# Later bias additions on the residual, and a later turn of the bias vectors, in a cross-attention block

## The chip, the cores and the metric

The kernel runs on one core of one Trainium2 chip. The metric is the device time in microseconds of one execution; lower is better. The engines are TensorE (PE in the profile; PEld is its weight load), VectorE (DVE), ScalarE (ACT), GpSimd (POOL) and SyncE (SP), which issues nearly all DMAs.

## The reference, cut to what matters

All data are float32. There are 8 sequences of 256 tokens, for the queries and for the context, and the width is 512.

```python
x = layer_norm(hidden, ln1_w, ln1_b)
q = x @ q_w + q_b            # 16 heads of 32
k = enc @ k_w + k_b
v = enc @ v_w + v_b
a = softmax(q @ k.T / sqrt(32), where(mask))  @ v
hidden = a @ cproj_w + cproj_b + hidden_states
y = layer_norm(hidden, ln2_w, ln2_b)
y = gelu(y @ fc_w + fc_b)    # 512 -> 2048
out = hidden + y @ proj_w + proj_b
```

## The kernel before

**Tiling.** Two sequences form a group of 512 tokens, so there are four groups, g = 0 to 3. Each matrix product is done in quarters of 256 by 256, named "11", "12", "21" and "22", by a Strassen scheme of seven products in place of eight (`strassen`, `fc`, `proj`); sums of quarters (`sum_up`, L171, `A_SUMS` for weights and `B_SUMS` for tokens) are made ahead of it on POOL and DVE. The first product of the keys of group 0 is the exception: `eight` makes each quarter by plain products, 16 recorded matmuls in two halves i = 0 and 1.

**No scheduler.** The order of the source is the order of the instructions on each engine. Each engine works off its own list in that order.

**Start.** Contexts, key weights, x and the other weights are loaded by SP. Eight small loads on POOL's queue bring the bias and norm vectors into `rows`, as rows. `turn_cols` turns them on PE into `ps_cols` (L476) and DVE copies them to `cols` (L477), the per-partition scalars that nearly every later step uses: the keys' bias in `made` (ACT, L437), the norm's scale in `turn_x`. The source calls `turn_cols` after the products of quarter "11". The order that follows is: turn the second half of the context (`pct`), quarter "12" (`pkT_12`), statistics of x on DVE (L194, L195), `roots` on POOL (L199, L200), quarter "21", the norm on DVE (L203), the transposes of x (`pxt`), quarter "22", then the queries (`pqT`).

**Attention.** It has 32 units, n = 0 to 31: eight per group, u = 0 to 7, each with four heads of one sequence. Unit n computes scores two units ahead, softmax on DVE and ACT, the division by the sums on POOL one unit ahead (`divide(n + 1)`, L599, `pr`, which waits for `rsum`, L597), turns the probabilities on PE (`ppt`, L610) and multiplies them by the values (`av`, L626). The lists `between` and `aside` hold other work for places inside a unit: `begin(g, u, i, f, ...)` puts f at place i of unit u of group g, where i = 0 to 2 lie before `attend` and i = 3 is the end of the unit. In these places the projections of the next group, the norms and the output projection (`project_out`, `po`) are woven in.

**The residual in the attention.** `load_res(g, n)` loads a quarter of x into `resx` by SP. The output projection adds its result to that tile on POOL (L541), and SP stores it to `hid_dram` (L542). For quarter "12" `load_res` also adds the difference `cbd` of two halves of the bias, on POOL (L534), in the same call as the load. Group 0's quarters are loaded at the end of unit 8, group 1's "12" at the end of unit 22, group 2's at the end of unit 28, and group 3's after unit 31.

**The MLP.** For each group, four steps q = 0 to 3 make a quarter of the hidden layer each: seven products (`pf`, L903), sums on DVE, GELU on ACT (L966), then two sums on POOL (L1007, L1008). In group 0, step q also makes the weight sums `fcw[q + 1]` of the following step on POOL. Step 0 loads the residual `resm` from `hid_dram` (1 MB, `residual`), adds two bias terms to halves of it on POOL (L1014), and loads the next group's tokens `hm` (`load_hid`). In group 0 SP issues this load after the four quarters of `proj_w` (`pw`, 1 MB each). After step 3 come the statistics of `hm` on DVE, `ve_m` and `rstd_m` on POOL, the norm on DVE (L203), and the output products (`proj`, `py`), between which `hm` is turned (`pyt`, `turn_next`). POOL makes sums for them (L1058, L1067), DVE empties the first product's bank (L1052), and the residual enters at L1064, L1075, L1080, L1083 and L1087.

Of the kernel before, what the change touches and what calls it, by code (L numbers as in the profile page):

```python
# [13 lines left out]
ALU = mybir.AluOpType  # L14
# [8 lines left out]
def tile_xattn_block(  # L23
# [45 lines left out]
    nc = tc.nc  # L69
# [6 lines left out]
    NG = B // GB  # L76
# [9 lines left out]
    HI, HC, HF, HD2 = INNER // 2, NC // 2, NF // 2, D // 2  # L86
# [37 lines left out]
    def col(base, i):  # L124
        return cols[:, base + i : base + i + 1]
# [42 lines left out]
    def sum_up(eng, x, table, *which):  # L168
        for i in which:
            to, a, b, op = table[i]  # L170
            eng.tensor_tensor(x[to], x[a], x[b], op)  # L171

    def load_tiles(pool, src, tag, name, between=None):
        tiles = []
        for t in range(NT):
            if between and t == NT // 2:
                between()
            xt = pool.tile([P, D], F32, tag=tag, bufs=NT, name=f"{name}_{t}")
            nc.sync.dma_start(xt, src[ts(t, P), :])
            tiles.append(xt)  # L180
        return tiles

    def group_of(x, g):
        return x[g * G : (g + 1) * G, :]
# [44 lines left out]
    def residual(pool, src, tag, name):  # L229

        t = pool.tile([P, NT, D], F32, tag=tag, bufs=1, name=name)
        nc.sync.dma_start(t, src.rearrange("(t p) d -> p t d", p=P))
        return t
# [3 lines left out]
    def load_hid(g):  # L237
        hids[g] = load_tiles(both, hid_dram[g], "xt", f"hm_{g}")
# [10 lines left out]
    with ExitStack() as att:  # L249
        work = att.enter_context(tc.tile_pool(name="attwork", bufs=2))  # L250
        cb = work.tile([P, D], F32, tag="cb", bufs=1, name="cb")
        cbd = work.tile([P, S], F32, tag="cbd", bufs=1, name="cbd")
# [4 lines left out]
        mbias, ctxT, xnT, vs, qk, probs, stats, res = ({} for _ in range(8))  # L257
# [16 lines left out]
        def turned(name):  # L274


            places[0] += 1
            if not pts and (places[0] % 2 or probs):
                return ps_t.tile([P, G], F32, tag="pt", name=name)
            return ps_s.tile([P, G], F32, tag="s", name=name)  # L280
# [64 lines left out]

            return [lambda c=c: piece(c) for c in range(NC)]

        turns, later = [0], []

        def strassen(name, a, b, weight_moves, made, bias=None):  # L350

# [103 lines left out]
        def eight(name, n, w, x, made):  # L455


            bank = ps_m.tile([P, 2, S], F32, tag=f"m{turns[0]}", name=f"{name}_{n}")
            turns[0] ^= 1
            for i in range(2):  # L460
                for c in range(NC):
                    nc.tensor.matmul(  # L462
                        bank[:, i, :],
                        w[f"{n[0]}{c // HC + 1}"][:, c % HC, ts(i, P)],
                        x()[f"{c // HC + 1}{n[1]}"][:, c % HC, :],
                        start=i == 0 and c == 0,
                        stop=c == NC - 1,
                        skip_group_check=True,
                    )
            if n == "11":  # L470
                turn_cols()
            made(n, bank, None)

        def turn_cols():
            ps = turned("ps_cols")
            nc.tensor.transpose(ps[:, :n_rows], rows, ident[:n_rows, :n_rows])  # L476
            nc.vector.tensor_copy(cols, ps[:, :n_rows])  # L477
# [41 lines left out]
        def by_tiles(row):  # L519
            return row[:, None, :].to_broadcast([P, 2, S])  # L520

        def quarter_of(src, n):

            o, k = int(n[0]) - 1, int(n[1]) - 1
            return src[k * S : (k + 1) * S, ts(o, S)].rearrange("(t p) d -> p t d", p=P)

        def load_res(g, *which):
            for n in which:
                r = work.tile([P, 2, S], F32, tag=f"res{n}", bufs=1, name=f"resx_{g}_{n}")
                nc.sync.dma_start(r, quarter_of(group_of(xf, g), n))  # L530
                res[g, n] = r
                if n == "12":

                    nc.gpsimd.tensor_tensor(r, r, by_tiles(cbd), ALU.add)  # L534

        def project_out(g):
            def made(n, bank, u):
# [119 lines left out]
        def begin(g, u, i, f, *args):  # L657
            aside[g, u, i].append(lambda: f(*args))
# [44 lines left out]
        def share(g, pieces, plan):  # L703

            pieces = list(pieces)
            for u, i, n in plan:
                between[g, u, i] += pieces[:n]
                del pieces[:n]
            assert not pieces
# [37 lines left out]
        spread(0, [(6, 2), (6, 2), (7, 2), (7, 2)], [lambda i=i: sum_up(GP, ws["c"], A_SUMS, i) for i in ALL])  # L747
        g = 1
        begin(g, 0, 3, load_res, 0, *QUARTERS)
        g = 2  # L750
        begin(g, 0, 3, spill_att, 1)
        begin(g, 5, 3, reload_att, 1)
        sums_at(att_in, 1, [(g, 6, 1), (g, 6, 2), (g, 7, 1), (g, 7, 2)])
        begin(g, 5, 3, load_res, 1, "11", "22", "21")
        begin(g, 6, 3, load_res, 1, "12")
        g = NG - 1
        share(
            g,
# [3 lines left out]
        for u, h, which in (  # L762
            (2, 2, ("11",)), (3, 2, ("22", "21")), (4, 2, ("12",)), (5, 3, ("11",)), (7, 3, ("22", "21"))
        ):
            begin(g, u, 3, load_res, h, *which)

        begin(g, 0, 0, load_hid, 0)
        norm_over(
# [20 lines left out]
        def run(pieces):  # L789
            for p in pieces:  # L790
                p()
# [19 lines left out]
        k, q, v, tx = project_qk(0, "kT"), project_qk(0, "qT"), project_v(0), turn_x(0)  # L811
# [67 lines left out]
        for i in ALL:  # L879
            run(o[i : i + 1])  # L880
            sum_up(V, ys[0], B_SUMS, i)
        run(o[4:])
        run(later)
        load_fc(3)
# [2 lines left out]
    with ExitStack() as mlp:  # L887
# [39 lines left out]
        for g in range(NG):  # L927
# [28 lines left out]
            for q in range(HF // 2):  # L956
                bank = {
                    n: ps_f.tile([P, 2, S], F32, tag=f"f{n}", name=f"pf{n}_{g}_{q}") for n in (1, 6, 7, 5)
                }
                u1 = work.tile([P, 2, S], F32, tag="u1", bufs=1, name=f"u1_{g}_{q}")  # L960
                u2 = work.tile([P, 2, S], F32, tag="u2", bufs=2, name=f"u2_{g}_{q}")
                u3 = work.tile([P, 2, S], F32, tag="u3", bufs=1, name=f"u3_{g}_{q}")

                def gelu(n, half, src):
                    for i in range(2):
                        nc.scalar.activation(  # L966
                            h[n][q][:, i, :],
                            src[:, i, :],
                            AF.Gelu_apprx_tanh,
                            bias=col(c_fcb, half * HF + 2 * q + i),  # L970
                            scale=1.0,
                        )

                ahead = g == 0 and q + 1 < HF // 2

                def some_pw(n):
                    if g == 0 and q:
                        for _ in range(n):
                            next(pw_sums)

                fc(bank[1], "11", "11", q, True, False)
                nc.scalar.copy(u1, bank[1])  # L982
                fc(bank[6], "s2", "t2", q, True, True)
                nc.vector.tensor_tensor(u2, bank[6], u1, ALU.add)
                fc(bank[7], "s3", "12", q, True, False)
                nc.vector.tensor_tensor(u3, bank[7], u2, ALU.add)
                fc(bank[5], "21", "t1", q, True, False)
                nc.vector.tensor_tensor(h["22"][q], bank[5], u3, ALU.add)
                if ahead:
                    sum_up(nc.gpsimd, fcw[q + 1], A_SUMS, 0, 1)  # L990
                some_pw(1)
                fc(bank[1], "12", "21", q, False, True)

                gelu("11", 0, bank[1])
                gelu("22", 1, h["22"][q])
                fc(bank[7], "22", "t4", q, False, True)
                nc.vector.tensor_tensor(h["12"][q], bank[7], u2, ALU.add)
                if ahead:
                    sum_up(nc.gpsimd, fcw[q + 1], A_SUMS, 2, 3)
                some_pw(2)  # L1000
                gelu("12", 1, h["12"][q])
                fc(bank[5], "s4", "22", q, False, True)
                nc.vector.tensor_tensor(h["21"][q], bank[5], u2, ALU.add)  # L1003
                some_pw(1)
                gelu("21", 0, h["21"][q])

                nc.gpsimd.tensor_tensor(h["s3"][q], h["11"][q], h["21"][q], ALU.subtract)  # L1007
                nc.gpsimd.tensor_tensor(h["21"][q], h["21"][q], h["22"][q], ALU.add)  # L1008
                if q == 0:
                    ht = residual(work, hid_dram[g], "resm", f"resm_{g}")  # L1010

                    for b, bias in ((0, projb[:, :HD2]), (1, pbd)):
                        o = out_quarter(b, 0)
                        nc.gpsimd.tensor_tensor(o, o, by_tiles(bias), ALU.add)  # L1014
                    if g + 1 < NG:
                        load_hid(g + 1)

            if g + 1 < NG:
                seen, roots, normalise = layer_norm(hids[g + 1], f"m{g + 1}")
# [3 lines left out]
            bank = {  # L1023
                n: ps_f.tile([P, 2, HD2], F32, tag=f"f{n}", name=f"py{n}_{g}") for n in (1, 6, 7, 5)
            }
# [104 lines left out]
```

## Time and profile before

| what | value |
|---|---|
| median of 3 runs | 768.07 us (766.93 to 768.81) |
| profiled execution, its own time | 769.02 us |
| span of that execution, first to last instruction | 767.2 us |
| PE busy | 749.7 us, 98% of the span |
| POOL, DVE, ACT busy | 378.3, 360.5, 293.0 us |
| mean granted PE clock | 0.993 |
| moved by DMA | 68.70 MB |

The span is what the engines' instructions cover. The difference of 1.8 us between span and time lies around it. A line of a timeline has start, duration, engine, source line, operation, output and inputs, shape and count; a bracket at its end gives the engine's idle time before it and what ended that. A line of waits has the waiting engine and line, what it waited for, then total, number and longest. PE's busy time has modelled ends, so consecutive pieces overlap by some 0.16 us.

### The profile page before, as it was taken

The page shows a single profiled execution, that of the slowest core. Times are in us where ns is not written, and L with a number is a line of the kernel's source. Part 1 is how long each engine was busy: PE and PEld are TensorE (multiplying, and loading weights), DVE is VectorE, ACT ScalarE, POOL GpSimd, SP SyncE. Part 2 cuts the span into 40 slices and gives each one's busy share as a digit, 9 for nine tenths or more (in the row PEclk, how much of TensorE's full clock was granted, in tenths as well). Part 3 has the DMA queues.
Part 4 walks back from the last instruction along what each step waited for, and adds up shares of the span by engine and source line. Part 5 has one row for each costly group of instructions (what it writes and reads, how often), then busy time and mean ns, then how long its engine had stood idle before and what let it go on. Part 6 is the DMA issues. An engine that isn't in the chain of part 4 may idle for free.

```text
span 767.2 us, 12111 instructions
## 1 busy us (share of the span) xinstructions
PE 749.7 (98%) x4437; PEld 628.9 (82%) x4437; DVE 360.5 (47%) x970; ACT 293.0 (38%) x851; POOL 378.3 (49%) x346
## 2 busy tenths in 40 slices
PE   8999999899999999999979999999999999999997
PEld 7888777688888777768858888888888888888886
DVE  3676756566466566765325641225512264122111
ACT  2277787655776777761313001330004210032100
POOL 3856779467564569986472530315403245022340
PEclk9999999999999999999989999999999999999999
DMA  9614432632234358333920004000031000110001
GB/s 302 223 56 147 147 111 84 187 119 83 83 101 152 96 180 283 116 97 98 309 102 1 1 0 152 14 0 1 1 100 65 1 1 0 59 52 0 1 1 55
DMA packets 60331, 68.70 MB, mean 90 GB/s; under 512 B 5060, under 2 KB 46064, under 8 KB 60144
## 3 DMA queue, kind: packets, MB, share of 16 engines
q1 hardware_dynamic: 60016, 67.91, 27.2%
q8 instruction: 35, 0.57, 0.3%
q14 instruction: 24, 0.20, 0.1%
q0 software_dynamic: 256, 0.02, 0.0%
HBM read 46.95 MB, written 20.97 MB: 89 GB/s over the span
## 4 chain that ended last, share of the span: by engine, by line
PE 84%; POOL 6%; issue 3%; DMA 2%; ACT 2%; DVE 1%; SPq 1%; POOLq 0%; DVEq 0%
PE py L903 25%; PE pf L903 23%; PE ppt L610 5%; PE pqT L367 5%; PE pkT L367 5%; PE pv L367 5%; PE po L367 5%; PE s L557 4%; PE av L626 4%; POOL pr L599 3%; DMA resm<-hid_dram 2%; PE pkT L462 1%; ACT pr L585 1%; PE pxt L216 1%; PE pyt L216 1%
## 5 line engine op out<-in xcount | busy, mean ns | idle before, releaser
L903 PE MATMUL pf<-y,fcw 128*128 128x256 f32 x896 | 196.9, 383 | 5.7 <-POOL fcw L171 5.7
L903 PEld LDWEIGHTS pf<-y,fcw 128*128 128x128 f32 x896 | 172.0, 192 | 30.0 <-POOL fcw L171 6.1
L599 POOL TENSOR_TENSOR pr<-pr,rsum 128x512 f32<-128x512 f32 x128 | 130.1, 1048 | 68.3 <-DVE rsum L597 44.8
L585 ACT ACTIVATE pr<-pr,nmax 128x256 f32<-128x256 f32 x256 | 128.1, 503 | 61.3 <-DVE nmax L575 61.2
L575 DVE CUSTOM_DVE_ANT_0 pr<-s,mb 128x256 f32<-128x256 f32 x256 | 94.0, 412 | 42.1 <-PE s L557 35.0
L1007 POOL TENSOR_TENSOR hs<-h,h 128x512 f32<-128x512 f32 x16 | 20.3, 1270 | 181.2 <-PE pf L903 139.0
L903 PE MATMUL py<-pw,h 128*128 128x256 f32 x384 | 84.8, 379 | 0.0
L903 PE MATMUL py<-pw_t,h 128*128 128x256 f32 x384 | 83.5, 379 | 0.0
L903 PEld LDWEIGHTS py<-pw,h 128*128 128x128 f32 x384 | 72.7, 190 | 9.8
L903 PEld LDWEIGHTS py<-pw_t,h 128*128 128x128 f32 x384 | 72.7, 190 | 9.8
L982 ACT COPY u<-pf 128x512 f32<-128x512 f32 x16 | 9.4, 586 | 165.9 <-PE pf L903 164.6
L610 PE MATMUL ppt<-ident,pr 128*128 128x128 f32 x512 | 69.1, 277 | 3.3 <-POOL pr L599 3.3
L610 PEld LDWEIGHTS ppt<-ident,pr 128*128 128x128 f32 x512 | 57.2, 141 | 18.4 <-issue 9.1
L966 ACT ACTIVATE h<-pf,cols 128x256 f32<-128x256 f32 x32 | 13.4, 470 | 108.3 <-PE pf L903 108.3
L615 ACT COPY pt<-ppt 128x512 f32<-128x512 f32 x96 | 51.6, 571 | 7.9 <-PE ppt L610 7.9
L966 ACT ACTIVATE h<-h,cols 128x256 f32<-128x256 f32 x96 | 43.4, 501 | 25.8 <-DVE h L1003 13.3
L367 PE MATMUL pqT<-xnT,qw 128*128 128x256 f32 x224 | 52.6, 388 | 0.0
L367 PE MATMUL pv<-vw,ctxT 128*128 128x256 f32 x224 | 52.4, 380 | 0.0
L585 ACT ACTIVATION_READ_ACCUMULATOR pr<-pr,nmax 128x1 f32 x256 | 48.5, 189 | 0.0
L367 PEld LDWEIGHTS pqT<-xnT,qw 128*128 128x128 f32 x224 | 42.5, 195 | 5.4
L367 PEld LDWEIGHTS pv<-vw,ctxT 128*128 128x128 f32 x224 | 41.0, 190 | 5.4 <-issue 0.3
L626 PE MATMUL av<-pt,v 128*32 128x256 f32 x512 | 38.9, 386 | 1.3 <-ACT pt L615 0.4
(132 smaller groups left out, 964.8 us busy)
## 6 DMA issues: line engine op xcount, KB each, us to landing
ctx<-in_ctx_dram SPq DMA_DIRECT2D x16, 256.0 KB, 4.3
x<-in_x_dram SPq DMA_DIRECT2D x16, 256.0 KB, 3.9
v_dram<-st_v SPq DMA_DIRECT2D x16, 256.0 KB, 2.2
v<-v_dram SPq DMA_DIRECT2D x16, 256.0 KB, 3.8
resx<-in_x_dram SPq DMA_DIRECT2D x16, 256.0 KB, 5.1
hid_dram<-resx SPq DMA_DIRECT2D x16, 256.0 KB, 2.2
hm<-hid_dram SPq DMA_DIRECT2D x16, 256.0 KB, 6.0
fcw<-in_L_xattn_fc_w_dram SPq DMA_DIRECT2D x16, 256.0 KB, 6.0
```

Of the source, the lines that this page charges most:

```text
L216: nc.tensor.transpose(ps[:, ts(t, P)], xt[:, ts(c, P)], ident)
L367: nc.tensor.matmul(bank[n][:, i, :], l[:, c, ts(i, P)], r[:, c, :], start=first and i == 0 and c == 0, stop=last and c == HC - 1, skip_gro ...
L557: nc.tensor.matmul(banks[j][:, i, :], qT[j * HD : (j + 1) * HD, b * S + i * P : b * S + (i + 1) * P], kT[j * HD : (j + 1) * HD, b * SK : ( ...
L575: nc.vector.tensor_tensor_reduce(pr[:, j, i, :], banks[j][:, i, :], mbias[g][1][:, b, :], scale=-SCALE, scalar=FLT_MAX, op0=ALU.add, op1=A ...
L585: nc.scalar.activation(pr[:, j, i, :], pr[:, j, i, :], AF.Exp, bias=nmax[:, j, i : i + 1], scale=-1.0, accum_out=sums[:, j, i : i + 1],)
L599: nc.gpsimd.tensor_tensor(pr[:, j], pr[:, j], rsum[:, j, :, None].to_broadcast([P, NQ, SK]), ALU.mult,)
L610: nc.tensor.transpose(ps[:, kc, ts(i, P)], probs[n][:, j, i, ts(kc, P)], ident)
L615: nc.scalar.copy(pt, ps)
L626: nc.tensor.matmul(av[j * HD : (j + 1) * HD, :], vs[g, hg][:, b * NK + kc, ts(j, HD)], pts[n, j][:, kc, :], start=(kc == 0), stop=(kc == N ...
L903: nc.tensor.matmul(ps, lhsT, rhs, start=first, stop=last, skip_group_check=True)
L966: nc.scalar.activation(h[n][q][:, i, :], src[:, i, :], AF.Gelu_apprx_tanh, bias=col(c_fcb, half * HF + 2 * q + i), scale=1.0,)
L1007: nc.gpsimd.tensor_tensor(h["s3"][q], h["11"][q], h["21"][q], ALU.subtract)
```

## The change

Three things move, and nothing is computed otherwise. Firstly, the addition of `cbd` to `resx` "12" leaves `load_res` for a function of its own, `bias_res`, called one or more units later (for group 3: after the fourth product of its output projection). Secondly, in the MLP the two additions of the bias to `resm` go from step 0, behind the load, to step 3; the loads stay in step 0. Thirdly, `turn_cols` is called between the two halves of the keys' quarter "12", and only then quarter "11" gets its bias.

```diff
-        turns, later = [0], []
+        turns, later, waiting = [0], [], []
...
             for i in range(2):
+                if n == "12" and i == 1:
+
+                    turn_cols()
+                    waiting.pop()()
                 for c in range(NC):
                     nc.tensor.matmul(
...
             if n == "11":
-                turn_cols()
-            made(n, bank, None)
+                waiting.append(lambda: made(n, bank, None))
+            else:
+                made(n, bank, None)
...
                 res[g, n] = r
-                if n == "12":
-
-                    nc.gpsimd.tensor_tensor(r, r, by_tiles(cbd), ALU.add)
+
+        def bias_res(g):
+
+            r = res[g, "12"]
+            nc.gpsimd.tensor_tensor(r, r, by_tiles(cbd), ALU.add)
...
         begin(g, 0, 3, load_res, 0, *QUARTERS)
+        begin(g, 2, 2, bias_res, 0)
...
         begin(g, 6, 3, load_res, 1, "12")
+        begin(g, 7, 3, bias_res, 1)
...
             begin(g, u, 3, load_res, h, *which)
+        begin(g, 6, 2, bias_res, 2)
...
             sum_up(V, ys[0], B_SUMS, i)
+        bias_res(3)
         run(o[4:])
...
                 if q == 0:
                     ht = residual(work, hid_dram[g], "resm", f"resm_{g}")
+                    if g + 1 < NG:
+                        load_hid(g + 1)
+                if q == HF // 2 - 1:
 
                     for b, bias in ((0, projb[:, :HD2]), (1, pbd)):
                         o = out_quarter(b, 0)
                         nc.gpsimd.tensor_tensor(o, o, by_tiles(bias), ALU.add)
-                    if g + 1 < NG:
-                        load_hid(g + 1)
```

## The prediction

> **What bounds the kernel now.** I read the page's busy shares first, then who TensorE (PE) waits for, then the timelines around each of those waits.
>
> ```profile
> PE 749.7 (98%) x4437; PEld 628.9 (82%) x4437; DVE 360.5 (47%) x970; ACT 293.0 (38%) x851; POOL 378.3 (49%) x346
> ```
>
> PE is the bound: it is idle for only 767.2 - 749.7 = 17.5 us. So an edit pays only where PE pauses, or where it runs slowly. The waits of PE alone:
>
> ```profile
> PE pf L903 <- POOL fcw L171: 5.7, 1, 5.7
> PE ppt L610 <- POOL pr L599: 3.3, 5, 2.0
> PE warm L796 <- POOL neg_half L110: 1.4, 1, 1.4
> PE ps_cols L476 <- DMA rows<-in_L_xattn_fc_b_dram: 1.1, 1, 1.1
> ```
>
> Three of the four belong to what the change touches. POOL's timeline (start, duration, line, last the idle time before) says why POOL was late with `fcw`, in MLP group 0:
>
> ```profile
> 377.29 1.27 POOL L1008 TENSOR_TENSOR h<-h,h 128x512 f32<-128x512 f32 x1
> 388.65 1.26 POOL L1014 TENSOR_TENSOR resm<-resm,projb 128x512 f32<-128x512 f32 x1 [10.09 <-DMA resm<-hid_dram]
> 389.87 1.26 POOL L1014 TENSOR_TENSOR resm<-resm,pbd 128x512 f32<-128x512 f32 x1
> 391.08 5.17 POOL L171 TENSOR_TENSOR fcw<-fcw 128x512 f32<-128x512 f32 x4
> ```
>
> The bias adds on `resm` wait 10.09 us for a load that SP issued behind 4 MB of `pw`; the `fcw` sums for the third step stand behind them. The same picture in unit 8 to 10 of the attention, where the add on `resx_12` stands ahead of the softmax divisions:
>
> ```profile
> 149.60 1.27 POOL L534 TENSOR_TENSOR resx<-resx,cbd 128x512 f32<-128x512 f32 x1 [9.64 <-DMA resx<-in_x_dram]
> 150.82 8.03 POOL L599 TENSOR_TENSOR pr<-pr,rsum 128x512 f32<-128x512 f32 x8
> ```
>
> A pause costs more than its length. In the windows (busy time of each engine, then the granted PE clock) PE is fully busy after each pause, but at a little over half rate:
>
> ```profile
> 149.00:153.00 4.00, 1.68 (x21) 1.04 (x15) 2.33 (x9) 1.36 (x5) 3.40 (x4) 1.00 0.57 193
> 153.00:157.00 4.00, 4.00 (x13) 3.32 (x14) 1.05 (x6) 1.57 (x5) 4.00 (x5) 0.57 0.95 339
> ...
> 394.00:400.00 6.00, 6.00 (x17) 4.82 (x18) 0.69 (x1) 0.00 (x0) 5.92 (x5) 0.58 0.00 0
> 400.00:406.00 6.00, 6.00 (x30) 5.28 (x29) 2.83 (x5) 1.63 (x4) 4.26 (x4) 1.00 0.00 0
> ```
>
> **What the Trainium skill says.** "TensorE: Matmul & The Clock Gate", Part 1, says that an idle array drops to half clock and needs a busy window of about 3.4 us to return. The trace agrees on the size (0.57, 0.58), but here a pause of some 2 us followed by a shorter one was enough. The same page (the note on queue depths) calls GpSimd's queue strict FIFO: agreed, the `fcw` sums waited behind `resm`. "SBUF — State Buffer", Who interferes with whom, says that a VectorE tensor_scalar in its two-port mode and a GpSimd instruction exclude each other: agreed, L203 takes 1.48 us beside POOL's L1058 and 0.54 us at 17.2, where POOL is idle.
>
> **The change part by part.** No DMA is issued in another order. Moved are 4 adds on `resx_12`, 8 on `resm`, one transpose with its copy, and two activations.
>
> *MLP.* The two adds go from step 0 to step 3. After L1008 ends at 378.5 POOL runs the four `fcw` sums (5.17) by 383.7; PE asks for the first of them at 388.0. The next ones follow L1007/L1008 of step 1, whose input ACT finishes at 388.0, so they are half done at about 393 against a need at 400.1. So nothing is late next. Gain: in the chain of work PE needs, from 362.10 to 419.08, 56.98 us for the four steps; in a group without a pause 48.35 (469.18 to 517.52). That is **8.63**: 5.74 of pause and 2.89 of half clock.
>
> Cost: in step 3 the adds (2 x 1.24 = 2.48) now stand before `ve_m`, `rstd_m` and L1058 in all four groups. Group 1:
>
> ```profile
> 521.85 0.23 POOL L199 TENSOR_SCALAR ve_m<-mv_m 128x4 f32<-128x4 f32 x1
> ...
> 523.24 5.71 DVE L203 TENSOR_SCALAR hm<-hm,mv_m,rstd_m 128x512 f32<-128x512 f32 x4 [1.78 <-POOL rstd_m L200]
> 528.87 0.68 DVE L1052 TENSOR_TENSOR v<-py,projb 128x512 f32<-128x512 f32 x1
> ```
>
> L203 now ends at 528.95 + 2.48 = 531.43; PE transposes `hm` from 531.17 and wants the last tile, after three transposes of 0.11, at 531.50. L1052 ends at 532.03, and PE reuses its bank at 532.05. So cover is used up to the last 0.05; in group 0, with 2.22 of delay (POOL had waited 0.26 for `mv_m`), L1052 ends at 433.7 against 433.6. I take 0.3 for three groups; bounds 0 and 1.5 (0.5 each). The delayed L1058 ends at 531.1 and is needed at 539.8; group 3 has no norm. DVE's `pw` sums and copies queued behind L203 in group 0 end at 437.6, needed at 440.5.
>
> *Attention, `resx_12` of group 0.* Its add goes behind `rstd_a` of unit 10. Then the divisions of unit 10 run once `rsum` is there (141.4) and end at 145.4, for a need at 149.7. What PE loses now: the transposes should have led to the first matmul of `pkT` 1.73 after 150.66, at 152.39; it came at 156.82. Gain **4.43**, of it 1.58 half clock (3.31 for 8 matmuls that take 1.73). The add itself (1.27) falls at about 160.7 to 162.0 on the new time scale, before the next `rsum` (166.5 - 4.4 = 162.1). Its load, landed at 149.6, is no issue.
>
> *Group 2's `resx_12`* (unit 28 to unit 30): before, POOL stood from 332.49 to 334.90 for it (the page blames DVE's `nmax`, but the load issued at 331.53 took 3.3 us), and PE then waited 0.56 in unit 30 and 0.33 + 0.56 in unit 31 for divisions. Afterwards they start 3.6 us sooner. Gain **1.45**. Group 1's add had waited 0.6 with no pause of PE: nothing. Group 3's add waited 7.4 at 358.5 under the last `po` products; PE had no pause there, so nothing, only that the last store goes some 0.5 sooner.
>
> *Start.* The bias transpose moves into the second key quarter. PE saves the 1.06 wait for `rows`: `pkT_12` starts about 11.2 instead of 12.55. But its copy to `cols` now waits for half of that product (11.2 + 1.73 + 0.27), and `bn_stats` of x stands behind it on DVE:
>
> ```profile
> 12.41 0.68 DVE L194 BATCH_NORM_STATS2 st_a<-x 128x6 f32<-128x512 f32 x1
> ...
> 17.18 1.92 DVE L203 TENSOR_SCALAR x<-x,mv_a,rstd_a 128x512 f32<-128x512 f32 x4 [1.49 <-POOL rstd_a L200]
> ```
>
> So the norm starts at 13.27 and ends at 19.96 instead of 19.10. PE is ready at 18.3 and transposes x as it comes, to end at 21.4 (before: 21.3). The 1.06 saved turn into a wait for DVE. I take **+0.1**; bounds -0.5 (the norm's chain shrinks) and +1.7 (the pause trips the clock). The two activations end at 14.3, before `pkT_21` needs their bank at 14.8.
>
> Sum: -8.63 - 4.43 - 1.45 + 0.3 + 0.1 = -14.1. The profiled execution took 769.02 (1.82 around its span); it becomes 754.9. It stands 0.95 above the median of 768.07, so I forecast **754.0**.
>
> **The rivals.**
> - *The start trips the clock.* Of the 1.7 us from 18.3, some 1.4 are idle. For it: about 2 us did at 149.9. Against: 1.06 and 0.35 close together at 9.9 to 12.5 did not. Price +1.6: 755.6.
> - *A moved wait isn't the one that ends last*, so that the change does not do what it says at that place: a late `rsum` or a filled queue keeps the divisions back (758.4 without the 4.43), or the `fcw` sums are late for another reason (762.6 without the 8.63). For it: the page's releasers are inferred, and one of them is wrong here. Against: the sums' start is the adds' end in the timelines.
> - *Slower: the adds and `bn_stats` exclude each other* at each end of a group. Then `ve_m` is late by 2.48 and another 4 x 0.66, 5.1 in all; with a cover of 2.3 PE pauses 2.8, and the clock adds up to 2.9: 5.7 in three groups, 17.1 against 14.5 won: 770.8. It decides from 4.8 per group on. Against: L1007 and L1008 already run beside `bn_stats` (518.2 to 521.4) at 1.27 and 0.66, as alone.
>
> **How the numbers follow.** The forecast 0.75 (its own range 752.5 to 755.5: 1.0 for the spread of 766.93 to 768.81, 0.5 for the start), the start 0.12, a wait that stays 0.10, slower 0.03. The range 752.5 to 759.0 takes in the first two and the 758.4. About 0.3%, 2.3 us, is what a measurement of this kernel can tell from no change: faster 0.95, same 0.02, slower 0.03.
>
> **What would show it.** Right: no PE wait for `fcw`, PE clock 1.0 through steps 1 to 3 of MLP group 0, about 48.4 from its first `pf` to its first `py`; no PE pause at 149 and 337 to 345; in the first 25 us, PE waiting for `x` from L203 in place of `rows`; L203's end within 0.1 of the `pyt` transposes. Wrong: a wait of PE for `hm` or `pyt` over 0.5 per group, POOL's adds above 1.5, a clock under 0.9 near 20.

## The result: 11.5 us faster

The changed kernel takes **756.0 us** (median of 4 runs, 755.8 to 756.3) against 767.5 us before (4 runs beside it, 766.9 to 768.8). The ratio is 0.985, 95% interval 0.983 to 0.987: 11.5 us less, between 10 and 13. The profiled executions differ a little more: their spans are 767.2 and 754.0 us, 13.2 apart.

Parts 1 and 4 of the page of the changed kernel, the busy times and the shares of the chain that ended last:

```profile
PE 745.0 (99%) x4437; PEld 625.1 (83%) x4437; DVE 361.2 (48%) x970; ACT 293.4 (39%) x851; POOL 380.2 (50%) x346
...
PE 94%; ACT 2%; DVE 2%; issue 1%; DMA 1%; POOL 0%; SPq 0%; DVEq 0%; POOLq 0%
```

PE has the same 4437 matmuls and is idle for 9.0 us where it was for 17.5. It is also busy for 4.7 us less with the same work: for the most part that is half clock that is gone. POOL's work has not shrunk (380.2 against 378.3), but its share of the chain rounds to 0%. What PE alone waits for now:

```profile
PE warm L806 <- POOL neg_half L110: 1.4, 1, 1.4
PE pkT L466 <- DMA kw<-in_L_xattn_k_w_dram: 0.9, 1, 0.9
...
PE pxt L216 <- DVE x L203: 0.2, 1, 0.2
```

The waits for `fcw`, for `pr` and for `rows` are off the list. In their place stands a short one for `x`. POOL's timeline in the first steps of MLP group 0 shows why; the `fcw` sums follow the sums of their own step at once:

```profile
372.28 1.27 POOL L1019 TENSOR_TENSOR h<-h,h 128x512 f32<-128x512 f32 x1
373.51 5.65 POOL L171 TENSOR_TENSOR fcw<-fcw 128x512 f32<-128x512 f32 x4
```

The same windows as before, which had 0.57 and 0.58 in the column of the granted clock (the second pair lies some 5 us further on in the work, since group 0 starts 5.0 sooner):

```profile
149.00:153.00 4.00, 4.00 (x34) 3.44 (x35) 3.57 (x15) 2.59 (x9) 0.93 (x1) 1.00 0.55 169
153.00:157.00 4.00, 4.00 (x24) 3.59 (x23) 3.75 (x14) 2.74 (x9) 3.12 (x4) 1.00 0.80 287
...
388.00:394.00 6.00, 6.00 (x29) 5.28 (x28) 4.29 (x6) 2.54 (x6) 3.24 (x3) 1.00 0.00 0
394.00:400.00 6.00, 6.00 (x30) 5.28 (x29) 2.15 (x4) 1.49 (x3) 2.53 (x2) 1.00 0.00 0
```

PE is busy for all of each window, at full clock. For the sum I cut the span at fixed pieces of PE's work. The same cuts serve for the experiments: the start up to the first `pqT`; from the scores that PE computes within unit 10 (those of unit 12) to the ones within unit 16; from the scores computed within unit 29 (the last ones) to the first `pf`; the four steps of MLP group 0; and the output products of groups 0, 1 and 2 with the norm between them (first `py` to the next `pf`).

| kernel (span, us) | start | unit 10 to 16 | unit 29 to `pf` | steps of group 0 | `py` of groups 0, 1, 2 |
|---|---|---|---|---|---|
| before (767.2) | 24.76 | 68.03 | 32.81 | 56.98 | 50.09, 50.10, 50.10 |
| after (754.0) | 24.98 | 63.75 | 31.83 | 48.35 | 50.30, 50.22, 50.21 |
| difference | +0.22 | -4.28 | -0.98 | -8.63 | +0.21, +0.12, +0.11 |
| predicted | +0.1 | -4.43 | -1.45 | -8.63 | +0.3 in all |

The differences add up to -13.2, the whole of the spans' difference.

### The profile page after: what moved, and what is told of

The parts are those of the page before. It is cut to its first block, busy times and chain, and to the rows that moved or that the text cites. A ratio compares the mean times of both kernels' runs of the same rounds, so it can differ in the third digit from the quotient of the medians.

```text
span 754.0 us, 12115 instructions
## 1 busy us (share of the span) xinstructions
PE 745.0 (99%) x4437; PEld 625.1 (83%) x4437; DVE 361.2 (48%) x970; ACT 293.4 (39%) x851; POOL 380.2 (50%) x346
## 4 chain that ended last, share of the span: by engine, by line
PE 94%; ACT 2%; DVE 2%; issue 1%; DMA 1%; POOL 0%; SPq 0%; DVEq 0%; POOLq 0%
PE py L914 26%; PE pf L914 26%; PE ppt L617 7%; PE pqT L367 6%; PE pv L367 5%; PE po L367 5%; PE s L564 5%; PE av L633 5%; PE pkT L367 5%; ACT pr L592 2%; PE pkT L466 1%; PE pyt L216 1%; PE pxt L216 1%; ACT pt L622 1%; PE pct L216 1%
## 5 line engine op out<-in xcount | busy, mean ns | idle before, releaser
L914 PE MATMUL pf<-y,fcw 128*128 128x256 f32 x896 | 194.0, 379 | 0.0
L914 PEld LDWEIGHTS pf<-y,fcw 128*128 128x128 f32 x896 | 170.2, 190 | 23.1
L367 PE MATMUL pqT<-xnT,qw 128*128 128x256 f32 x224 | 51.0, 379 | 0.0
```

The costliest lines, as they stand in the source:

```text
L367: nc.tensor.matmul(bank[n][:, i, :], l[:, c, ts(i, P)], r[:, c, :], start=first and i == 0 and c == 0, stop=last and c == HC - 1, skip_gro ...
L914: nc.tensor.matmul(ps, lhsT, rhs, start=first, stop=last, skip_group_check=True)
```

## The experiments

The theory is that of the prediction: additions at the head of POOL's queue held up the sums and divisions that PE needed, each pause made PE run on at half clock, and nothing else decides the time. Its rivals: the half-clock stretch has a cause of its own; the additions and `bn_stats` hold each other up; the start matters in itself.

### One part at a time

Three kernels that take over one part each, the others as before.

**e1_mlp_only**: only the additions on `resm` move.

```diff
-                if q == 0: [adds on resm]
+                if q == HF // 2 - 1: [adds on resm]
```

> The kernel before with the MLP part alone: the adds on resm go to step 3. Theory (the pause for fcw and the half clock behind it go, the norm's cover at the ends of groups 0 to 2 is just used up): span 8.63 - 0.43 = 8.2 us shorter than before, about 759; group 0 from first pf to first py 48.4, then 0.1 to 0.2 more per group before the fourth output product. Rival (part of the 8.63 belongs to the earlier stores and loads that the attention part brings): the pause shrinks but stays, 3 to 6 us won, and PE still waits for fcw or hs.

Measured: 760.7 us (758.8 to 761.4), ratio 0.989 (0.986 to 0.993), 7.1 less than the kernel before beside it (767.7), where 8.2 was expected. The steps of group 0 take 48.35, as in the whole change. The profiled execution is the fastest of the four (758.8), and in it unit 10 to 16 takes only 65.52 although nothing was changed there; its clock held at 1.00 behind that pause, as it does in e12 below.

**e2_resx_only**: only the additions on `resx` "12" move (`bias_res`).

```diff
-                if n == "12":
-                    nc.gpsimd.tensor_tensor(r, r, by_tiles(cbd), ALU.add)
+        begin(g, 2, 2, bias_res, 0)   # and groups 1, 2, 3
```

> The kernel before with bias_res alone, at its four places. Theory: unit 10 gains 4.3 and units 30 and 31 gain 1.0, so the span is 5.3 shorter, about 762, and the pause for fcw with its half clock stays at 8.6. Rival (the gain in units 30 and 31 is the 1.45 of the forecast, and was only lost again elsewhere): 5.9 shorter.

Measured: 763.6 us (763.0 to 765.8), ratio 0.995 (0.993 to 0.996), 4.1 less. Unit 10 to 16 takes 63.75 and the last units 31.83, as in the whole change; group 0's steps still 56.58. So both gains are there in the profile (4.28 and 0.98, the 5.3 that was expected), while the medians show 1.2 less; the two gains are taken against the first profile of before, in which unit 10 lost its full price (e12).

**e3_cols_only**: only `turn_cols` moves.

```diff
+                if n == "12" and i == 1:
+                    turn_cols()
+                    waiting.pop()()
```

> The kernel before with the later turn of the bias vectors alone. Theory (the wait for rows becomes a wait for the norm of x, since the copy to cols stands ahead of bn_stats on DVE): the first pqT starts at about 25.1 in place of 24.9, span within 0.3 of before. Rival (the wait for kw that the run after showed at 5.9 hid a gain of 0.9): first pqT at about 24.2, 0.7 shorter.

Measured: 768.2 us (765.7 to 770.1), ratio 1.000 (0.998 to 1.002). The first `pqT` came at 25.51. In the profiled executions with the old order it came at 24.76, 25.15, 25.23, 25.27 and, in e2_resx_only, at 27.13; with the new order at 24.98 to 25.80, so no sooner. The third part moves the median by nothing that can be told. The one late start is half clock again. PE's timeline and a window of e2_resx_only:

```profile
11.63 0.23 PE L476 MATMUL ps_cols<-ident,rows 44*128 44x44 f32 x1 [1.54 <-DMA rows<-in_L_xattn_fc_b_dram]
...
13.23 8.86 PE L462 MATMUL pkT<-ctxT,kw 128*128 128x256 f32 x32 [0.35 <-DVE ctxT L324]
```

```profile
13.00:17.00 4.00, 3.77 (x10) 3.10 (x11) 3.24 (x9) 0.51 (x1) 0.44 (x2) 0.59 1.11 338
```

The wait for `rows`, 1.54 here, is followed by products at 0.59, which take 8.86 for 7.17. So the old order could lose 1.7 at this place when `rows` came late; none of the profiled executions with the new order did.

The two parts that pay give 7.1 + 4.1 = 11.2 of the 11.5. These medians are known to within some 2.7 and 1.4 us only; that neither part hides the other is shown by the stages, each of which is as short with one part alone as in the whole change.

### Is the half clock the pause's doing?

**e4_before_fill**: the kernel before, with 40 transposes of the identity into an unused bank, in the place where PE pauses for `fcw`. They are work that the output doesn't need.

```diff
                 nc.scalar.copy(u1, bank[1])
+                if g == 0 and q == 2:
+                    dummy = ps_m.tile([P, G], F32, tag="mm", name="dummy")
+                    for t in range(40):
+                        nc.tensor.transpose(dummy[:, ts(t % NT, P)], ident, ident)
```

> The kernel before with 40 transposes of the identity on PE, into a bank that nobody reads, ahead of the second product of step 2 in MLP group 0, where PE pauses 5.74 us; they take about 4.3 us. Theory (the slow matmuls after the pause are the clock that drops because PE idles): with the pause filled the clock stays at 1.0, no slow matmuls, span 2.9 shorter though PE does more. Rival (they are slow for what runs beside them, POOL's sums or the loads of weights just made): still 2.9 of slow matmuls, span as before within 0.5.

PE's timeline there, and the windows of the same kernel:

```profile
388.23 4.53 PE L986 MATMUL dummy<-ident 128*128 128x128 f32 x40
393.16 9.12 PE L903 MATMUL pf<-y,fcw 128*128 128x256 f32 x41 [0.40 <-POOL fcw L171]
```

```profile
388.00:394.00 6.00, 5.60 (x46) 5.19 (x45) 0.07 (x1) 1.00 (x3) 5.82 (x5) 1.00 0.15 56
394.00:400.00 6.00, 6.00 (x30) 5.28 (x29) 2.73 (x4) 0.00 (x0) 5.84 (x6) 1.00 0.00 0
```

`fcw` comes 4.93 us after PE has done all that it could do without it (393.16 - 388.23), yet the clock stays at 1.00 and the steps of group 0 take 53.38, against 56.58 to 56.98 in the kernels with the bare pause. With 40 more instructions PE is 3.2 to 3.6 us sooner. Not all of that is clock: the bare pauses are a little longer, 5.11 to 5.74 (before, e2, e3, e12). What these four lose beyond the pause, against 48.35, is 2.7 to 3.1 us; in e4 it is 0.1 (53.38 - 48.35 - 4.93). So the half clock comes from PE standing idle, not from what it runs afterwards. The total follows in part: 765.8 (763.4 to 767.6), ratio 0.997 (0.995 to 0.998), 1.9 less than before; what became of the rest I did not find.

### How much cover is left, and do the additions and `bn_stats` collide?

**e8_four_adds**: the changed kernel with each addition on `resm` followed by one more of the same size into a spare tile, whose result is not used.

```diff
                         nc.gpsimd.tensor_tensor(o, o, by_tiles(bias), ALU.add)
+                        nc.gpsimd.tensor_tensor(spare, o, by_tiles(bias), ALU.add)
```

> The changed kernel with each add on resm in step 3 followed by one more of the same size into a tile that nobody reads: 2.5 us more on POOL at the end of each group. Theory (the cover of the norm is used up by the first 2.5): all of it shows, PE stops 2.4 to 2.5 us before the pyt transposes in groups 0 to 2, 7.4 in all, and the clock drops behind stops of that length, 1.6 to 2.9 more each: span 9 to 16 longer than the changed kernel. Rival (there is still cover): under 4 longer, clock 1.0.

The waits of PE alone (first line), two windows at the end of group 0, and PE's first products after that:

```profile
PE pyt L216 <- DVE hm L203: 6.5, 6, 1.1
```

```profile
419.00:423.00 4.00, 1.85 (x11) 1.11 (x10) 4.00 (x4) 0.00 (x0) 3.20 (x3) 1.00 0.00 0
423.00:427.00 4.00, 4.00 (x13) 3.25 (x12) 3.92 (x7) 0.00 (x0) 0.00 (x0) 0.57 0.00 0
```

```profile
423.19 8.76 PE L914 MATMUL py<-pw,h 128*128 128x256 f32 x32
```

Two more additions of 1.27 make every group 4.3, 4.3 and 4.1 us longer (54.61, 54.47, 54.27 in place of 50.30, 50.22, 50.21): 6.5 / 3 = 2.2 of waiting, and then the clock; 32 products take 8.76 where they took 7.17. The median is 767.2 us (765.1 to 769.4), ratio 1.000: **the whole gain is gone**. The first two additions had used up nearly all of the cover. The mechanism of the slower rival had no place to act. POOL's and DVE's timelines at the end of group 0:

```profile
409.01 1.27 POOL L1020 TENSOR_TENSOR h<-h,h 128x512 f32<-128x512 f32 x1
409.57 0.66 DVE L194 BATCH_NORM_STATS2 st_m<-hm 128x6 f32<-128x512 f32 x1
410.24 1.27 POOL L1029 TENSOR_TENSOR resm<-resm,projb 128x512 f32<-128x512 f32 x1
```

The last `bn_stats` ends at 410.23, and the first addition on `resm` starts at 410.24; in groups 1 and 2 too the additions come after them all. What does run beside `bn_stats` is the pair of sums ahead of the additions (L1019, L1020), and neither is slowed: 1.27 and 0.66.

**e5_adds_step2**: the additions of the changed kernel one step earlier, in the third step (`if q == 2:`), where POOL has room and the load has long landed.

> The changed kernel with the adds on resm in step 2 in place of step 3. Theory (the adds in step 3 delay the norm by 2.5 us, 0.1 more than its cover): PE's stops at the pyt transposes and at the third output product go, 0.43 shorter in the span, L203 ends 2.5 earlier against PE; resm has landed by then, so POOL does not wait. Rival (the 0.43 comes from elsewhere, as the sharing between POOL and DVE): within 0.1.

The three groups take 50.10 each, as before the change: the 0.44 is given back. The median, 756.0 (755.3 to 756.2), ratio 0.985 (0.983 to 0.987), doesn't show it; in the profiled execution the start took 25.80, 0.8 more than in that of the changed kernel.

### What stood behind the wait in the last units

**e7_av_bank**: in units 29 and 30 `av` takes a bank from the scores' pool, which makes no scores any more there, in place of the two-bank pool that it shares with `ppt`.

```diff
-            av = ps_t.tile([P, S], F32, tag="pt", name=f"av_{n}")
+            if n in (29, 30):
+                av = ps_s.tile([P, G], F32, tag="s", name=f"av_{n}")[:, :S]
+            else:
+                av = ps_t.tile([P, S], F32, tag="pt", name=f"av_{n}")
```

> The changed kernel with the av result of units 29 and 30 in a bank of the scores' pool, which has no scores left to hold by then. Theory (in units 30 and 31 the second group of ppt waits until ACT has emptied av out of the shared pair of banks, since no scores stand between): the eight ppt of these units take 1.09 again in place of 1.35 and 1.38, 0.5 shorter. Rival (they wait for the divisions on POOL): unchanged.

PE's timeline of the changed kernel, the first group of transposes in the last two units that turn ahead, and the instruction of ACT that the first of them meets:

```profile
333.20 1.35 PE L617 MATMUL ppt<-ident,pr 128*128 128x128 f32 x8
333.30 0.47 ACT L641 ACTIVATE att<-av,cols 128x256 f32<-128x256 f32 x1 [0.15 <-PE av L633]
...
338.96 1.38 PE L617 MATMUL ppt<-ident,pr 128*128 128x128 f32 x8
```

And in e7_av_bank:

```profile
333.88 1.09 PE L617 MATMUL ppt<-ident,pr 128*128 128x128 f32 x8
...
339.38 1.10 PE L617 MATMUL ppt<-ident,pr 128*128 128x128 f32 x8
```

Eight transposes take 1.04 when nothing holds them. In the changed kernel they took 0.3 more twice: the second four waited for ACT to empty the bank of `av` (L641, 0.47 us, which starts only when `av` is done). With another bank that goes, and the stage takes 31.27 in place of 31.83. The median is 755.9 (755.3 to 756.0): 0.56 was not to be told from the changed kernel in the time, with a start of 25.59 against 24.98 in the profiled executions.

### How large is the pause of unit 10, really?

**e9_undo_first_resx**: the changed kernel, with only group 0's addition on `resx` back behind its load.

```diff
                 res[g, n] = r
+                if n == "12" and g == 0:
+                    bias_res(0)
...
-        begin(g, 2, 2, bias_res, 0)
```

> The changed kernel with group 0's bias_res called by load_res again (unit 8). Theory: unit 10 loses what the landing of resx_12 and the clock make of it in this execution, 1.8 (a short pause, clock kept) to 4.3 us (clock dropped), nothing else moves: 757.8 to 760.3. Rival (the load's landing does not set it): the same loss in each execution.

Measured: 760.5 us, its four runs at 758.06, 760.53, 760.79 and 760.46, ratio 0.991 (0.989 to 0.992). So this one addition is worth some 4.5 us of the medians. The profile was taken of the fastest of them, and in it the stage is only 1.72 longer (65.47 against 63.75), with a granted clock of 1.00. The three others were granted 0.997 on average, and are 2.5 us longer. A drop of the clock behind this pause explains some 1.6 of that (8 products took 3.31 for 1.73 in the kernel before); the rest may be a longer pause, but there is no profile of them.

**e12_before_again**: the kernel before, unchanged, profiled a second time.

> The kernel before once more, for a second profile. Theory: the span from unit 10 on and the four steps of MLP group 0 differ from the first profile, since the pauses hang on when loads land and the clock drops or not; all other stretches agree within 0.1. Rival: they agree too, and what varies between executions is the start alone.

It took 767.1 us, with a stage of 65.84 where the first profile had 68.03. PE's timeline and the window after the pause:

```profile
151.98 0.66 PE L610 MATMUL ppt<-ident,pr 128*128 128x128 f32 x4 [1.46 <-POOL pr L599]
```

```profile
153.00:157.00 4.00, 4.00 (x21) 3.54 (x22) 2.71 (x13) 1.58 (x5) 4.00 (x5) 1.00 1.02 356
```

The same instructions paused for 1.46 us in place of 2.0, and the clock didn't drop: 2.2 us less in this stage, 0.4 less in the steps of group 0 (56.58). One kernel, one stage, two prices: 2.1 us where the clock held, 4.3 where it dropped. The expectation left out that the start differs too, 25.27 against 24.76.

### Better than both

**e6_cols_first_half**: the changed kernel, with `turn_cols` ahead of the whole quarter "12".

```diff
-                if n == "12" and i == 1:
+                if n == "12" and i == 0:
```

> The changed kernel with the turn of the bias vectors ahead of the first half of the keys' quarter 12, not between its halves. Theory (the copy to cols holds up bn_stats on DVE): bn_stats starts at about 11.5, PE doesn't wait for x, the first pqT starts 1.0 to 1.3 earlier than in the changed kernel, and the span is that much shorter. Rival (x lands too late, between 10.7 and 12.5, so the norm can't start earlier): bn_stats waits for x, at most 0.4 shorter.

PE's timeline at the start:

```profile
18.80 1.91 PE L216 MATMUL pxt<-ident,x 128*128 128x128 f32 x16
...
24.01 7.29 PE L367 MATMUL pqT<-xnT,qw 128*128 128x256 f32 x33
```

DVE's statistics start at 12.02 in place of 13.31, the transposes of x no longer wait for DVE, and the first `pqT` comes 0.97 sooner; 754.6 us (754.4 to 755.0), ratio 0.983 (0.982 to 0.985), below every run of e5 and e7, which ran on the same chip. PE waited 0.76 for `rows` in this execution, less than the 1.06 before.

**e10_all_three**: e5, e6 and e7 together.

> The changed kernel with the adds on resm in step 2, the turn of the bias vectors ahead of the first half of quarter 12, and av of units 29 and 30 in the scores' pool. Theory: the three gains lie at different places of PE's work and add: 0.43 + 1.0 to 1.4 + 0.5, so 2.0 to 2.3 shorter than the changed kernel, about 753.8. Rival (they overlap): that of the turn alone, 754.5.

Span 752.0; each stage shows its own gain at once (23.77, 63.76, 31.28, 48.34, 50.10 three times). The median is **753.7 us** (753.6 to 754.0), ratio 0.982 (0.980 to 0.983): the best of all, 2.3 below the changed kernel (measured at another time; against the kernel before, the ratios are 0.982 and 0.985).

**e11_stats_ahead**: e5 and e7, with `turn_cols` where the change has it, and the statistics of x put ahead of its copy on DVE.

```diff
-        run([first[0], k[0], first[1], k[1]])
+        run([first[0], k[0], first[1], *seen, k[1]])
...
-        run([*seen, roots, k[2], *normalise])
+        run([roots, k[2], *normalise])
```

> The changed kernel with the adds on resm in step 2, av of units 29 and 30 in the scores' pool, and the statistics of x issued ahead of the keys' quarter 12, so that on DVE they stand ahead of the copy to cols, which stays between the halves. Theory (the wait is one of queue order on DVE): bn_stats starts at about 11, the norm ends by 18, PE waits neither for rows nor for x, first pqT at about 23.5 to 24.3, 753.3 to 754. Rival (the copy to cols now comes late, at about 14, and pkT_21 waits for its bank): as with the turn in the first half or worse.

The statistics start at 11.06 and the norm ends at 17.74, a microsecond before PE asks for x. It gave 754.3 us (754.1 to 754.4), ratio 0.983 (0.981 to 0.984): a little above the 753.3 to 754 that were expected, and 0.6 above e10, on the same chip. Two ways out of the same wait, and the simpler is as good. What makes the 0.6 I did not find: in the profiled executions the starts (24.12 and 23.77) differ by 0.35.

## Why the prediction was right, and where it was off

The sign, and the mechanism behind each of the two large terms, were right. Forecast: 754.0; measured: 756.0. That lies in the range of 752.5 to 759.0, but just outside the forecast's own 752.5 to 755.5.

**MLP: right to the last digit** in the profile: 48.35, and the clock at 1.00 through the windows of 388 to 400. The split, too, was of the right size: four executions with the bare pause lose 2.7 to 3.1 beyond it (e4), for the 2.89 of the prediction.

**Unit 10: 4.28 for 4.43.** POOL's timeline has the step as foreseen, the divisions at once, and the addition much later, behind `rstd_a`:

```profile
141.80 4.04 POOL L606 TENSOR_TENSOR pr<-pr,rsum 128x512 f32<-128x512 f32 x4 [1.56 <-ACT pr L592]
...
161.10 1.27 POOL L541 TENSOR_TENSOR resx<-resx,cbd 128x512 f32<-128x512 f32 x1
```

**The start: +0.22 for +0.1, by the chain that was foreseen.** That the two numbers are so close is luck, since the first `pqT` moves by 0.8 between executions of the new order. The wait for `rows` became one for DVE. DVE's timeline, then PE's:

```profile
13.31 0.68 DVE L194 BATCH_NORM_STATS2 st_a<-x 128x6 f32<-128x512 f32 x1
...
18.08 1.92 DVE L203 TENSOR_SCALAR x<-x,mv_a,rstd_a 128x512 f32<-128x512 f32 x4 [1.49 <-POOL rstd_a L200]
```

```profile
18.68 3.01 PE L216 MATMUL pxt<-ident,x 128*128 128x128 f32 x16 [0.15 <-DVE x L203]
```

The statistics start at 13.31 (predicted 13.27), the norm ends at 20.00 (19.96). The 16 transposes stretch to 3.01 in place of 1.91: most of the wait is hidden in them, and the list of waits, with its 0.2, shows only the first of it. The clock didn't drop there, so the rival that the start trips it was wrong; of the two orders it is the old one that did so (e2).

**The delay of the norm: +0.44 for +0.3**, inside its bounds. DVE's timeline of group 1, and the chain at the end of group 0:

```profile
512.27 5.71 DVE L203 TENSOR_SCALAR hm<-hm,mv_m,rstd_m 128x512 f32<-128x512 f32 x4 [4.24 <-POOL rstd_m L200]
```

```profile
419.26 0.98 PE pyt L216 x8
...
427.25 0.87 PE pyt L216 x8
```

The norm ends at 517.98, while PE turns its tiles from 517.75: the cover is used up to some tenths. In group 0 the first eight transposes stretch to 0.98, where the second eight, without a wait, take 0.87. e8 shows what lies past this edge.

**Units 30 and 31: 0.98 for 1.45.** The term that was mis-sized is this one: the divisions did come sooner, but behind them stood another wait that the prediction didn't name. e7 gives 0.56 back when it goes, and 0.98 + 0.56 = 1.54 is about what the prediction had taken for the whole.

These terms explain the profiled execution: 754.9 was predicted for it, and it took 755.8. Of the 0.9 between them, 0.47 is the last units, 0.15 unit 10, 0.14 the norm and 0.12 the start.

**The largest single miss is the last line of the sum**, "less 0.95" for the profile's distance to the median. It takes for granted that what the profiled execution had lost against the median stays lost or won in the same way afterwards. But that surplus was most likely in the pauses that the change removes. The mean granted clock of each execution of the kernel before speaks for it (all that were run beside the experiments):

| mean granted clock of the execution | 0.997 and 0.998 | 0.995 and 0.996 | 0.993 | 0.991 |
|---|---|---|---|---|
| executions | 4 | 24 | 27 | 4 |
| mean time, us | 764.8 | 766.8 | 768.4 | 770.9 |

The profile of before, 0.993 and 769.0, had both drops at full price; e12, at 0.996, lacked that of unit 10. The sizes fit: half clock lasted 6.8 us in all in e12 and 10.2 in before, and half of that is 0.4% and 0.7% of their spans. The changed kernel has no pause that trips the clock: 0.999 or 1.000, and its four runs lie within 0.5 us, with the profiled one 0.2 below their median. So there was nothing to subtract: 0.95 + 0.2 are the rest of the 2.0 by which the forecast was low. It is also why 13.2 between two profiles is 11.5 between medians.

**The rivals.** That an old wait isn't the last one was true in small, in the last units. The slower case could not come about as it was argued: the additions start when `bn_stats` has ended, and POOL's sums beside it are not slowed (e8). Its arithmetic was near: it put the point that decides at 4.8 us per group, of 14.5 won; with the 13.2 that were won it is 4.4, and e8, at 4.1 to 4.3, comes out level.

**The Trainium skill.** "TensorE: Matmul & The Clock Gate", Part 1, gives at least one idle window of about 3.4 us for the drop to half clock, and says that the window is free-running. On the first the runs differ: two waits of 1.07 and 1.08 us with one transpose between them were enough in e8. With the second they agree. Windows of e8, each pair just before and within one of its three drops, then of before:

```profile
422.70:423.05 0.35, 0.35 (x5) 0.35 (x4) 0.35 (x2) 0.00 (x0) 0.00 (x0) 1.00 0.00 0
423.10:426.45 3.35, 3.35 (x10) 2.69 (x9) 3.35 (x6) 0.00 (x0) 0.00 (x0) 0.50 0.00 0
525.10:525.45 0.35, 0.03 (x1) 0.04 (x1) 0.35 (x2) 0.00 (x0) 0.00 (x0) 1.00 0.00 0
525.50:528.85 3.35, 3.35 (x11) 2.90 (x12) 2.03 (x3) 0.00 (x0) 0.00 (x0) 0.50 0.00 0
627.50:627.85 0.35, 0.00 (x0) 0.00 (x0) 0.35 (x1) 0.00 (x0) 0.35 (x1) 1.00 0.00 0
627.90:631.25 3.35, 3.03 (x10) 2.67 (x11) 2.45 (x4) 0.00 (x0) 0.00 (x0) 0.50 0.02 5
```

```profile
153.35:156.70 3.35, 3.35 (x10) 2.69 (x9) 0.70 (x5) 1.57 (x5) 3.35 (x4) 0.50 0.96 350
392.30:399.05 6.75, 5.31 (x13) 4.24 (x14) 0.69 (x1) 0.00 (x0) 6.51 (x7) 0.50 0.00 0
```

Within a drop the clock is at one half, for 3.4 us or for twice that. In e8 the drops start 102.4 us apart both times, 30 times 3.41, although the output products of their groups start 102.95 and 102.82 apart; in before the two starts are 238.9 apart, 70 times 3.41. So the clock changes on a time grid of its own, and not a fixed time after a pause. That fits with length alone not deciding: the wait for `rows` tripped the clock with 1.54 us in e2, and not with 2.15 in e12. How much idle time within one stretch of the grid trips it is not settled by these runs.

## What to carry to other kernels

An addition whose operand comes by DMA belongs at the point of use, not behind its load: on an engine with one queue, all that stands behind it waits for the DMA as well. But look for the place with the most cover, not for the last one that works: here one step earlier costs nothing, and another 2.5 us in the chosen place cost the whole gain. And a pause that can trip the clock has no single price; read the granted clock of several executions before you subtract it, and don't carry a profile's distance to the median over into a kernel without those pauses.

## What the runs showed of the hardware

- A drop of TensorE's clock to one half lasted 3.4 us or twice that, and within an execution its starts lay whole multiples of 3.41 us apart (e8, before). Length alone did not decide: a wait of 1.54 us (e2) and two of 1.07 and 1.08 (e8) tripped it, waits of 1.46 and 2.15 us (e12) did not.
- The executions of one kernel fall into groups by their mean granted clock, 1.6 to 2.5 us apart (table above).
- Filling a pause of TensorE of some 5 us with useless transposes held the clock at 1.00 and made a stage 3.2 to 3.6 us shorter and the whole kernel 1.9 (e4).
- VectorE's `bn_stats` and GpSimd's additions on 128 x 512 f32 tiles don't slow each other: 0.66 and 1.27 us side by side (L194 beside L1020 in e8).
- The start differs between executions: PE waited up to 1.0 us for `kw` in some and not at all in others, and with one order of the instructions the first `pqT` came between 24.8 and 25.3 us, and at 27.1 where the clock had dropped.
